# A gather that also waits until the third gather ahead of it has landed

## The chip, the core and the metric

The kernel runs on one core of a Trainium2 chip. A core has five engines with instruction streams of their own: TensorE (PE, matrix products; PEld is its weight load), VectorE (DVE), ScalarE (ACT), GpSimd (POOL) and SyncE (SP), which only issues transfers here. They tell each other of finished work through semaphores. Sixteen DMA engines move data between HBM and the on-chip memory; they are shared by all transfers, whoever issued them. A transfer raises a semaphore when it has landed. The metric is the time of one execution on the device, in microseconds (us).

## The reference

The kernel computes one layer of attention over the edges of a graph with 12500 nodes and 212500 edges (sorted by target node), then a batch norm over the nodes, a residual and a layer norm. Cut to what matters:

```python
Q, K, V = (x @ W for W in (WQ, WK, WV))            # 12500 x 128, as 8 heads of 16
Eh = edge_attr @ WE                                # 212500 x 128
score = K[src] * Q[dst] / sqrt(16) * Eh            # rows of K by source, of Q by target
score = exp(clip(score.sum(per head), -5, 5))
msg = V[src] * score
h_attn = segment_sum(msg, dst) / (segment_sum(score, dst) + 1e-6)
h = x + h_attn
h = (h - mean) * rsqrt(var + 1e-5) * gamma + beta  # over the nodes
out = layernorm(x + h)                             # over the 128 features of a node
```

The edges' sources are in no order, so K[src] and V[src] have to be fetched row by row: for each edge 1 KB, the K row and the V row of its source beside each other.

## The kernel before, in words

**Tiles and groups.** The edges are cut into 1661 tiles of 128 and these into 208 groups of eight tiles (the last has five). A group is made of two halves of four tiles, one for each of two windows of 64 target nodes.

**The table.** A first stage computes K and V of all nodes on TensorE and writes them as a table `kvd` to HBM, one row of 1 KB per node. For the first eight groups x itself is gathered and projected, so that they need no table.

**The gathers.** `gather` (line 221) issues an indirect transfer on POOL: 128 row numbers from a column of `srcs`, 128 rows of `kvd`, one tile of a `slot` in the on-chip memory, 128 KB in all. One gather serves one tile. `load_kv` (line 296) puts the gathers of a group into the list `queued` once a slot is free, and `issue` (line 228) and `pace` (line 233) take them from there. In the steady loop `pace` makes the first of them wait for the last product that read the slot before; the others follow on POOL's queue. Each gather raises one of eight completion semaphores in turn, and each waits, before it starts, for the gather that used its semaphore last, the eighth ahead. Twelve of the groups get their last tile not by a gather but by 128 transfers of one row each from SP's queue (`fetch_rows`, line 270), eight rows in an iteration.

**The other transfers in the steady loop**, all from SP's queue: `load` (line 504) brings the edge attributes of a group, `ea`, 512 KB, four groups ahead, as soon as the products that read the buffer before (`eh_mm`, line 584) are done; `load_quad` (line 401) brings the target positions of four groups, `rbq`, in two transfers of 256 KB. Near the end `load_x` (line 488) brings x for the residual into slots that are no longer needed.

**The order.** The program writes the order of every engine by hand: the loop at line 842 calls one small function after the other for group g and its neighbours, and each engine runs its instructions in that order. For group g VectorE multiplies K in the slot by the turned product of Q and Eh (`products`, line 640), once for each half; each of the two instructions waits until the gathers of its tiles have landed. Then come the sums by head (line 647), clip and exp, and the message (`message`, line 662), after which the slot is free. TensorE adds the messages up by target node (line 679).

`steady[0] = True` (line 804) stands after the table is written and the first gathers have been issued, ahead of the loop over the attention groups.

Of the kernel before, what the change touches and what calls it, by code (L numbers as in the profile page):

```python
# [29 lines left out]
ROWS = P  # L30
FIRST_ROW = 8
LATE = 8
BATCH = 1
ROW_LAG = 2
SP_ROWS = 8
# [43 lines left out]
def gnn_kernel(  # L79
# [19 lines left out]
    nc = tc.nc  # L99
# [38 lines left out]
    srcs = consts.tile([P, T], I32, name="srcs")  # L138
# [65 lines left out]
    table = [False]  # L204
    steady = [False]
# [9 lines left out]
    def kv_view(g, t):  # L215
# [2 lines left out]
        KV[g] = lambda a, b, c, n=P: (v[:, a:b, c:c + n] if g not in by_row or b < G else  # L218
                                      by_row[g][:, :, c:c + n])

    def gather(out, table, e):
        return nc.gpsimd.indirect_dma_start(out=out, out_offset=None, in_=table,  # L222
                                            in_offset=bass.IndirectOffsetOnAxis(ap=srcs[:, e:e + 1], axis=0))


    queued = []
# [1 line left out]
    def issue(n=0):  # L228
        while len(queued) > n:
            f, *a = queued.pop(0)  # L230
            f(*a)

    def pace(step):
        if queued:
            f, *a = queued.pop(0)
            tc.add_manual_dep(f(*a).ins, step.ins.name,
                              mybir.DependencyInfo(mybir.DependencyClass.Sync, mybir.DependencyReason.DATA),
                              reason="pace")
# [57 lines left out]
    def load_kv():  # L296
        while free and pending and table[0]:
            g = pending.pop(0)
            i = free.pop(0)
            kv_view(g, (i, slot(i)))  # L300
            for j in range(sizes[g] - (g in by_row)):
                queued.append((gather, KV[g](j, j + 1, 0, 2 * P).rearrange("p a d -> p (a d)"), kvd,
                               starts[g] + j))
            if not steady[0]:
                issue()

    for g in range(nxg):
        if g % 2 == 0:
            PAIR[g // 2] = free.pop(0)
            t = slot(PAIR[g // 2])  # L310
        XG[g] = t[:, (g % 2) * G * P:(g % 2 + 1) * G * P].rearrange("p (g d) -> p g d", d=P)
        for j in range(G):
            queued.append((gather, XG[g][:, j, :], x, g * G + j))
# [38 lines left out]
    def within(f, g):  # L352
        return f(g) if 0 <= g < NG else None
# [55 lines left out]

    quads = range(-(-2 * LATE // RQ), sizes.count(G) // RQ)  # L410

# [20 lines left out]
    def norm_first():  # L432

        nc.vector.bn_aggr(pre[:, 1:3], stats[:, :NPRE, :])
        nc.vector.tensor_tensor(stats[:, NPRE - 1, 3:6], pre, npre, op=OP.mult)
# [406 lines left out]
    for g in range(NG - 2):  # L842
# [18 lines left out]
        within(q_mm, g + 4)  # L861
        if g < LATE + 4:
            issue()
        elif g % BATCH == 0:
            pace(SENT[g - 1])
# [26 lines left out]
        if g == NG - 5:  # L892
            assert done >= set(range(NPRE))
            norm_first()
        if g == LATE - 1:
            tps.close()
            late.append(tps.enter_context(tc.tile_pool(name="late", bufs=1)))
        if g == LATE - 2:
            free.append(NSLOT)
# [329 lines left out]
```

## Time and profile before

| | |
|---|---|
| time, median of 3 runs (lowest, highest) | 2130.77 us (2128.43, 2132.06) |
| the profiled execution: its time, its span | 2129.44 us, 2127.7 us |
| busy: TensorE, VectorE, ScalarE, POOL | 1710.7, 1590.3, 670.9, 1593.9 us |
| gathers from `kvd` on POOL | 1585, busy 1505.5 us |
| DMA: bytes, mean rate | 386.61 MB, 182 GB/s |
| DMA queues, share of 16 engines' span: gathers, SP's | 33.8%, 25.5% |

The span goes from the first to the last instruction of the program in the trace; the execution's own time is 1.7 us longer. "Busy" is the time in which an engine had an instruction at work, and it does not count waiting. A row of a group names the line, the engine, the operation, what it writes and reads and how often, then busy time and the mean of one in ns, then the engine's idle time just ahead of these instructions and what ended it; "issue" there means that no semaphore in the trace did. For a gather, POOL's busy time is the writing of the transfer's descriptors; the transfer itself runs later on the DMA engines. In a timeline a row gives start, duration, engine, line, operation, tiles and, in brackets, the idle time before it and what ended that.

### The profile page before, as it was taken

The numbers are of one execution on the slowest core, as the hardware profiler recorded it, in microseconds if no ns is written. First come the engines' busy times: TensorE is split into PE (matmuls) and PEld (weight loads), VectorE is DVE, ScalarE is ACT, GpSimd is POOL, SyncE is SP. The second block draws the span as 40 slices with busy tenths as digits, with TensorE's granted clock in tenths as the row PEclk, the third lists the DMA queues.
The fourth block names the chain that finished last, engine by engine and source line by source line (L and its number), as shares of the span: only waits on it lengthen the run. The fifth ranks groups of instructions, "written<-read, shape, count | busy, mean of one in ns | idle before, by whom it ended". The sixth has DMA issues, their size and how long they took to land. (4 is left out here: it accounts for less than half of the span.)

```text
span 2127.7 us, 34387 instructions
## 1 busy us (share of the span) xinstructions
PE 1710.7 (80%) x9414; PEld 1103.8 (52%) x9414; DVE 1590.3 (75%) x3593; ACT 670.9 (32%) x2688; POOL 1593.9 (75%) x1685
## 2 busy tenths in 40 slices
PE   8889999877787787777777887787787777877787
PEld 7566566544454454454444554455554444545456
DVE  4559999777777777777777777767777767777787
ACT  3344343322322322322322322223223223223226
POOL 7776777777777777777777777777777777777775
PEclk9999999999898999999999999998998999898999
DMA  9856666565565565565565565565555565565574
GB/s 302 285 183 186 203 195 198 175 176 167 164 182 170 176 175 166 169 182 172 169 176 173 168 177 165 177 174 168 176 175 167 174 176 167 174 178 163 180 236 130
DMA packets 175391, 386.61 MB, mean 182 GB/s; under 512 B 37518, under 2 KB 91831, under 8 KB 175191
## 3 DMA queue, kind: packets, MB, share of 16 engines
q0 software_dynamic: 78128, 212.05, 33.8%
q1 hardware_dynamic: 92900, 169.50, 25.5%
q10 hardware_dynamic: 4163, 2.78, 0.5%
q8 instruction: 78, 1.28, 0.2%
q14 instruction: 122, 1.00, 0.2%
HBM read 364.57 MB, written 19.63 MB: 181 GB/s over the span
## 5 line engine op out<-in xcount | busy, mean ns | idle before, releaser
L222 POOL DMA_INDIRECT slot<-kvd,srcs x1585 | 1505.5, 950 | 487.6 <-issue 460.5
L640 DVE TENSOR_TENSOR slot<-slot,ps_t 128x512 f32<-128x512 f32 (+1 forms) x410 | 274.1, 677 | 423.0 <-DMA slot<-kvd,srcs 355.6
L622 PE MATMUL ps_t<-ident,wt 128*128 128x128 f32 x1661 | 282.3, 312 | 361.6 <-DVE wt L614 358.7
L679 PE MATMUL ps_a<-msg,oh 128*128 128x136 f32 (+1 forms) x3322 | 527.1, 298 | 1.7 <-DVE msg L662 1.7
L622 PEld LDWEIGHTS ps_t<-ident,wt 128*128 128x128 f32 x1661 | 211.3, 159 | 537.3 <-issue 472.5
L679 PEld LDWEIGHTS ps_a<-msg,oh 128*128 128x128 f32 (+1 forms) x3322 | 427.7, 171 | 81.1 <-issue 53.9
L657 ACT ACTIVATE ps_m<-s 128x64 f32<-128x64 f32 (+1 forms) x209 | 47.5, 227 | 1097.3 <-DVE s L656 1003.6
L589 PE MATMUL ps_e<-ea,w_e 128*128 128x512 f32 x832 | 390.6, 591 | 0.7 <-ACT wt L596 0.7
L614 DVE TENSOR_TENSOR wt<-wt,ps_q 128x512 f32<-128x512 f32 x416 | 264.3, 675 | 2.6 <-PE ps_q L604 2.6
L647 DVE TENSOR_REDUCE s<-slot 128x64 f32<-128x1024 f32 (+2 forms) x208 | 246.3, 1185 | 0.1
L662 DVE TENSOR_TENSOR msg<-slot,ps_m 128x1024 f32<-128x1024 f32 (+3 forms) x209 | 246.0, 1179 | 0.3 <-ACT ps_m L657 0.3
L596 ACT ACTIVATE wt<-ps_e 128x512 f32<-128x512 f32 x416 | 233.8, 620 | 12.1 <-PE ps_e L589 12.0
L604 PE MATMUL ps_q<-ot,q 64*128 64x512 bf16 x1248 | 209.7, 451 | 0.0
L589 PEld LDWEIGHTS ps_e<-ea,w_e 128*128 128x128 f32 x832 | 142.6, 190 | 100.4 <-issue 98.5
L542 DVE TENSOR_TENSOR oh<-ps_m,rel_i 128x512 f32<-128x512 f32 x208 | 141.0, 678 | 10.8 <-PE ps_a L679 10.8
L570 ACT ACTIVATE q<-qs 128x128 bf16<-128x128 f32 x208 | 64.4, 309 | 214.9 <-PE ps_q L604 180.3
L704 PEld LDWEIGHTS ps_a<-ident,at 128*128 128x128 f32 x408 | 71.3, 218 | 110.4 <-ACT q L577 53.4
L704 PE MATMUL ps_a<-ident,at 128*128 128x128 f32 x408 | 114.3, 367 | 2.5 <-DVE relrow L396 2.3
L709 ACT ACTIVATE hx<-ps_a 128x64 f32 x408 | 88.0, 216 | 44.4 <-PE ps_a L679 37.5
L531 ACT ACTIVATE xw<-hx 128x64 f32 x416 | 88.1, 280 | 11.2 <-DMA kvd<-slot 6.5
L604 PEld LDWEIGHTS <-q 64*128 64x128 bf16 x1248 | 48.5, 102 | 79.0 <-issue 61.6
L562 PE MATMUL ps_a<-w_q,xw 128*128 128x128 f32 x416 | 88.9, 299 | 0.6 <-ACT qs L566 0.4
(180 smaller groups left out, 1632.0 us busy)
## 6 DMA issues: line engine op xcount, KB each, us to landing
ea<-eaT SPq DMA_DIRECT2D x207, 512.0 KB
slot<-kvd,srcs POOLq DMA_INDIRECT x1585
byrow<-kvd SPq DMA_DIRECT2D x1536, 1.0 KB
rbq<-relT SPq DMA_DIRECT2D x94, 256.0 KB
kvd<-slot SPq DMA_DIRECT2D x12, 512.0 KB
kvd<-t SPq DMA_DIRECT2D x12, 512.0 KB
slot<-xT SPq DMA_DIRECT2D x24, 256.0 KB
out<-o SPq DMA_DIRECT2D x23, 256.0 KB
```

The source lines that it names most:

```text
L222: return nc.gpsimd.indirect_dma_start(out=out, out_offset=None, in_=table, in_offset=bass.IndirectOffsetOnAxis(ap=srcs[:, e:e + 1], axis=0))
L542: nc.vector.tensor_tensor(one, iota_ps[:, None, :].to_broadcast([P, n, P]), r[:, :n, None].to_broadcast([P, n, P]), op=OP.is_equal)
L589: nc.tensor.matmul(eh, w_e, EA[g][:, a:b, :].rearrange("p a b -> p (a b)"), start=True, stop=True)
L596: nc.scalar.activation(t[:, :(b - a) * P], EH[g][h], AF.Copy)
L604: nc.tensor.matmul(QE[g][h], Q3[g][r, k, :], OT[g][r, :(b - a) * P], start=(k == 0), stop=(k == 2))
L614: nc.vector.tensor_tensor(t, t, QE[g][h], op=OP.mult)
L622: nc.tensor.transpose(ps[:, j, :], WT[g][h][:, j * P:(j + 1) * P], ident)
L640: step = nc.vector.tensor_tensor(kv, kv, PW[g][i][:, c - a:d - a, :], op=OP.mult)
L647: step = nc.vector.tensor_reduce(SS[g][:, a:b, :], KV[g](a, b, 0).rearrange("p t (h d) -> p t h d", d=DH), axis=AX.X, op=OP.add)
L662: step = nc.vector.tensor_tensor(MSG[g][:, a:b, :P].rearrange("p t (h d) -> p t h d", d=DH), KV[g](a, b, P).rearrange("p t (h d) -> p t h ...
L679: nc.tensor.matmul(AGG[g][WN if j >= n else 0:], OH[g][j], MSG[g][:, j, :], start=(j == 0), stop=(j == n - 1))
L704: nc.tensor.matmul(ps, AT[g], ident, start=True, stop=False)
```

## The change

`gather` keeps a list `flight` of the gathers issued since `steady` was set. From the fourth on, each gets a dependency on the one three places ahead in that list: it may start only when that one's data has landed. So at most three gathers are under way at a time. Nothing else is changed: the same instructions in the same order on every engine, the same transfers.

```diff
 LATE = 8
+FLIGHT = 3
...
+    flight = []
+
     def gather(out, table, e):
-        return nc.gpsimd.indirect_dma_start(out=out, out_offset=None, in_=table,
-                                            in_offset=bass.IndirectOffsetOnAxis(ap=srcs[:, e:e + 1], axis=0))
+        d = nc.gpsimd.indirect_dma_start(out=out, out_offset=None, in_=table,
+                                         in_offset=bass.IndirectOffsetOnAxis(ap=srcs[:, e:e + 1], axis=0))
+        if steady[0]:
+            flight.append(d)
+            if len(flight) > FLIGHT:
+                tc.add_manual_dep(d.ins, flight[-1 - FLIGHT].ins.name,
+                                  mybir.DependencyInfo(mybir.DependencyClass.Sync, mybir.DependencyReason.DATA),
+                                  reason="in flight")
+        return d
```

In the built program the new dependency takes the place of the wait on the eighth gather ahead, which it implies; the first five gathers that carry it keep both.

## The prediction

> **What bounds the kernel now.** I read the page first (busy time, groups, chain), then the groups of the gather line by its tile, then the waits, and last the timeline around single gathers.
>
> ```profile
> span 2127.7 us, 34387 instructions
> PE 1710.7 (80%) x9414; PEld 1103.8 (52%) x9414; DVE 1590.3 (75%) x3593; ACT 670.9 (32%) x2688; POOL 1593.9 (75%) x1685
> ...
> ACT 1%; PE 1%; DVE 0%; issue 0%; DMA 0%; POOL 0%; DVEq 0%; ACTq 0%
> ...
> L222 POOL DMA_INDIRECT slot<-kvd,srcs x1585 | 1505.5, 950 | 487.6 <-issue 460.5
> L640 DVE TENSOR_TENSOR slot<-slot,ps_t 128x512 f32<-128x512 f32 (+1 forms) x410 | 274.1, 677 | 423.0 <-DMA slot<-kvd,srcs 355.6
> ...
> ea<-eaT SPq DMA_DIRECT2D x207, 512.0 KB
> ...
> rbq<-relT SPq DMA_DIRECT2D x94, 256.0 KB
> ```
>
> ```profile
> L222 POOL DMA_INDIRECT slot<-kvd,srcs x1585: 942/946/1141, 83.3 to 2075.2; - x199
> ```
>
> ```profile
> POOL slot L222 <- issue: 475.4, 1560, 0.3
> ...
> DVE slot L640 <- DMA slot<-kvd,srcs: 355.6, 155, 6.8
> ```
>
> No engine is over 80% busy, and the chain on the page breaks off after a few per cent (its shares add up to 2), so it cannot name the bound. The gather line can. Its 1585 gathers start between 83.3 and 2075.2 us: 1991.9/1584 = 1.257 us from start to start. One takes 950 ns, and ahead of 1560 of them POOL is idle for 475.4/1560 = 0.30 us that no semaphore ends ("issue"). 0.95 + 0.30 = 1.25: POOL goes from gather to gather without waiting for anyone, for 94% of the span. The 75% is 0.95/1.257, an engine that is never free. VectorE in turn waits for the gathers (355.6 us, 155 times), TensorE for VectorE. So whatever delays a gather's start on POOL moves the end by as much; after the last gather 2127.7 - 2075.2 = 52.5 us of tail remain, which the change does not touch.
>
> **The change: what it adds.** No instruction, no transfer and no byte. In the instruction streams each gather of before already waits for the one eight ahead of it (eight completion semaphores in turn). In the changed stream this wait names the semaphore of the third ahead; only the first five carry both. So the 0.30 us between gathers, in which a wait is looked at already, gets no extra wait to look at: cost nothing by itself. Two edges would be a gather's own longer decoding (none seen) and the wait being open. The gathers before the first attention group (64 of x and the first 16 of K and V) keep their old order.
>
> **When the wait is open.** The third gather ahead started 3 x 1.25 = 3.75 us earlier. What counts is how long a gather takes from start to landing. VectorE shows it: its product L640 starts when the last gather of its four-tile half has landed.
>
> ```profile
> 387.62 0.94 POOL L222 DMA_INDIRECT slot<-kvd,srcs  x1 [0.30 <-issue]
> ...
> 390.47 0.69 DVE L640 TENSOR_TENSOR slot<-slot,ps_t 128x512 f32<-128x512 f32 x1 [2.65 <-DMA slot<-kvd,srcs]
> ...
> 577.02 0.95 POOL L222 DMA_INDIRECT slot<-kvd,srcs  x1 [0.30 <-issue]
> 577.37 0.36 SPq L507 DMA_DIRECT2D ea<-eaT  x1
> ...
> 581.25 0.69 DVE L640 TENSOR_TENSOR slot<-slot,ps_t 128x512 f32<-128x512 f32 x1 [1.85 <-DMA slot<-kvd,srcs]
> ...
> 555.89 1.25 SPq L405 DMA_DIRECT2D rbq<-relT  x2
> 556.96 0.94 POOL L222 DMA_INDIRECT slot<-kvd,srcs  x1 [0.31 <-issue]
> 564.12 0.69 DVE L640 TENSOR_TENSOR slot<-slot,ps_t 128x512 f32<-128x512 f32 x1 [6.09 <-DMA slot<-kvd,srcs]
> ...
> 750.13 0.94 POOL L222 DMA_INDIRECT slot<-kvd,srcs  x1 [0.30 <-issue]
> 750.19 1.25 SPq L405 DMA_DIRECT2D rbq<-relT  x2
> 755.85 0.69 DVE L640 TENSOR_TENSOR slot<-slot,ps_t 128x512 f32<-128x512 f32 x1 [1.08 <-DMA slot<-kvd,srcs]
> ...
> 1028.56 1.24 SPq L405 DMA_DIRECT2D rbq<-relT  x2
> 1029.65 0.95 POOL L222 DMA_INDIRECT slot<-kvd,srcs  x1 [0.30 <-issue]
> 1036.25 0.69 DVE L640 TENSOR_TENSOR slot<-slot,ps_t 128x512 f32<-128x512 f32 x1 [2.00 <-DMA slot<-kvd,srcs]
> ```
>
> (Which gather a product waits for: counted in eights from the last gather of the kernel, one less for each group that gets its last tile row by row.) With nothing beside it a gather has landed 390.47 - 387.62 = 2.85 us after its start: 0.9 us before the third after it wants to start, wait closed. Beside one ea load it took 4.23 us; beside an ea load and the two rbq loads behind it 7.16, 5.72 and 6.60 us, 6.5 in the mean.
>
> ```profile
> 1046.00:1047.25 1.25, 1.25 (x8) 0.71 (x7) 0.00 (x0) 0.00 (x0) 0.95 (x1) 1.00 0.36 105
> 1049.75:1051.50 1.75, 0.31 (x3) 0.34 (x4) 1.72 (x6) 1.32 (x7) 1.37 (x2) 1.00 0.85 267
> 1069.75:1074.25 4.50, 4.09 (x31) 3.11 (x32) 4.04 (x10) 2.25 (x9) 3.37 (x4) 1.00 1.00 284
> ```
>
> These three stretches (the last two columns are the DMA engines' busy share and GB/s) say why. A lone gather uses 0.36 x 1.25 = 0.45 us of the 16 engines. An ea load fills them for some 1.75 us (share 0.85), an ea load with two rbq loads for 4.5 us (share 1.00). A gather whose packets come behind such a block waits for it.
>
> How late after a landing does POOL start? The one true wait of a gather in the trace:
>
> ```profile
> 176.59 1.22 DVE L662 TENSOR_TENSOR msg<-slot,ps_m 128x1024 f32<-128x1024 f32 x1
> 178.07 0.94 POOL L222 DMA_INDIRECT slot<-kvd,srcs  x1 [4.87 <-DVE msg L662]
> ```
>
> 176.59 + 1.22 = 177.81, and 178.07 is 0.26 us later. The landings above are read at VectorE's start, which itself lies between 0 and some 0.26 us behind them, so the wait opens for landings read as longer than something between 3.75 - 0.26 = 3.49 and 3.75. I take 3.6, the middle.
>
> **The sum.** One block of loads stops POOL once: later gathers have come later, find the block gone, and one gather's 0.45 us is shorter than the 1.25 us between starts, so the queue drains.
> - rbq blocks: 94 loads, two to a block, so 47 blocks. 6.5 - 3.6 = 2.9 us by the three rows. Those have a gather in the worst place; with at most three in flight instead of five (6.5/1.25), there is also about one gather less (0.45 us) ahead in the queue. I take 2.5: 47 x 2.5 = 118 us.
> - ea loads without rbq: 207 - 47 = 160. The first gather to meet the block is late by 0.5 to 1.75 us (a gather comes every 1.25 us), so it lands after 3.35 to 4.60 us, in which the row of 4.23 lies. Over 3.6 this is 0 to 1.0 us, in the mean 1.0 x 1.0/(2 x 1.25) = 0.40: 160 x 0.40 = 64 us.
> - The last groups also load the residual's x, 25 loads of up to 256 KB in about six bursts:
>
> ```profile
> L494 SPq DMA_DIRECT2D slot<-xT x25: 327/424/1303, 2008.2 to 2066.9; - x25
> ```
>
>  At 2 us, a little under an rbq block: 6 x 2 = 12 us.
>
> Together 194 us. Nothing hides it: POOL has no idle time that the 0.30 us does not need. Behind a waiting gather stand the other gathers of its group and those of the next one, on POOL's queue; for them waits VectorE (L640), and for VectorE the transposes of TensorE and with them the release of ea buffers, so the next loads on SyncE's queue move back by about the same. TensorE and ScalarE lose nothing of their own; they wait longer. The profiled execution took 2129.4 us (span 2127.7): 2129.4 + 194 = 2323. The median of the runs, 2130.77, lies 1.3 us above that execution: 2325.
>
> **Weighed against the pages.** The row: landings of 2.85 us alone and 4.23 to 7.16 us beside loads. The Trainium skill, "DMA: Bandwidth & Descriptors", section "Anatomy of one DMA — SWDGE (gpsimd) path", gives a DMA of POOL's queue as 2.0 us plus its bytes by 436 GB/s, which is an estimate of 2.3 us for 128 KB whatever runs beside it; by that the wait would never be open and the time would stay. The trace agrees for a lone gather only, roughly. The same page, "Queues, rings and completion order", has each DMA engine take turns between queues packet by packet. By fair turns a gather beside a load would need about twice its 0.45 us, land after some 3.3 us, and again the wait would stay closed. The 4.23 us and 6.60 us speak against fair turns.
>
> **Rivals.**
> 1. The wait is never open (fair turns of the queues, or a dependency that ends up without force): 2131. For it: the lone landing of 2.85 us leaves 0.9 us. Against: the three landings over 5.7 us; of the 155 waits of VectorE the longest is 6.8 us.
> 2. The blocks shrink: fewer gathers in flight let the loads through sooner, so an rbq block costs 1.5 us, an ea load 0.25, an x burst 1: 47 x 1.5 + 160 x 0.25 + 6 = 116 us, 2247. For it: the gathers in a block use engine time that the loads then get. Against: in the 4.5 us at 284 GB/s 1278 kB move, and the three loads alone are 1049 kB of them, so without any gather the block still lasts some 3.7 us.
> 3. The blocks always catch a gather at the worst place, since POOL and the loads now move in step: 3.3 us for an rbq block (7.16 less 3.6, less 0.26 for VectorE's own start), 0.6 for an ea load, 3 for an x burst: 155 + 96 + 18 = 269 us, 2400.
> 4. Faster: the gathers write their descriptors undisturbed when fewer transfers run, each takes the shortest 942 ns instead of 950: 1585 x 0.008 = 12.7 us, 2118. It decides only where no landing goes beyond 3.5 us, since one rbq block in ten (5 x 2.5 = 12.5) eats it up. Against: the minimum and the median, 942 and 946 ns, lie together; there is little to win.
>
> **How the numbers follow.** My forecast has 0.66, rival 2 0.14, rival 3 0.12, rival 1 0.05, rival 4 0.03. Rivals 2 and 3 are the same mechanism with the ends of its prices; the range takes in both and a little beyond, 2235 to 2410, and leaves out rivals 1 and 4 and the far tails. About 0.2% is what a measurement of this kernel can tell from no change: faster 0.03, same 0.05, slower 0.92.
>
> **What would show it.** In the profile after: the group of the gather line keeps 950 ns but its idle time goes from 487.6 to some 680 us, the surplus named as waiting for the gather's own landing, 150 to 300 times, none over about 4 us. VectorE's wait for gathers grows by about the same from 355.6. Busy times of all engines stay. Between loads the gathers stay 1.25 us apart. Wrong would be: start to start longer than 1.25 us everywhere, which would make the wait itself costly (0.05 us more on 1566 gathers is 78 us); stalls beside ea loads over 1 us; or gathers that land after 2.85 us beside the loads too.

## The result, and the profile after

The changed kernel took 2383.02 us (median of 4 runs, 2376.3 to 2386.0) against 2129.82 us (4 runs, 2128.43 to 2132.06) for the kernel before: a ratio of 1.1185, with a 95% interval of 1.1172 to 1.1199. The forecast was 2325 us with a range of 2235 to 2410: the sign, the place and the range held, the middle was 58 us too low.

First the page of the kernel after: span, busy times, and the groups of the gather and of the VectorE product that waits for it (gather's line now 225, product's now 650).

```profile
span 2381.5 us, 34392 instructions
...
PE 1780.0 (75%) x9414; PEld 1145.7 (48%) x9414; DVE 1592.1 (67%) x3593; ACT 667.8 (28%) x2688; POOL 1592.0 (67%) x1685
...
L225 POOL DMA_INDIRECT slot<-kvd,srcs x1585 | 1503.6, 949 | 742.1 <-issue 398.4
...
L650 DVE TENSOR_TENSOR slot<-slot,ps_t 128x512 f32<-128x512 f32 (+1 forms) x410 | 276.2, 678 | 674.3 <-DMA slot<-kvd,srcs 589.0
```

The span grew by 2381.5 - 2127.7 = 253.8 us. POOL's idle time just ahead of the gathers grew by 742.1 - 487.6 = 254.5 us, and a gather still takes 949 ns. So the whole loss stands on POOL between two gathers, which is where the prediction had put it; it is only 254 us instead of 194.

The same gathers by their tile, and the waits (engine, what waited, for what; us in total, times, longest):

```profile
L225 POOL DMA_INDIRECT slot<-kvd,srcs x1585: 940/946/1217, 83.5 to 2327.9; - x199
```

```profile
DVE slot L650 <- DMA slot<-kvd,srcs: 589.0, 184, 8.2
...
POOL slot L225 <- issue: 414.9, 1301, 2.9
POOL slot L225 <- DMA slot<-kvd,srcs: 330.2, 317, 4.0
```

Where before no gather stood beyond the usual 0.30 us for another one, 317 now wait for one, for 330.2 us (0.30 us of each is the old pause), none longer than 4.0 us. VectorE's wait for the gathers grew from 355.6 to 589.0 us, 233 us of the 254. The median gather is as before, 946 ns. After the last gather 2381.5 - 2327.9 = 53.6 us remain, against 52.5.

Two stretches of the timeline show the two kinds of stall. First an rbq block:

```profile
1010.32 0.95 POOL L225 DMA_INDIRECT slot<-kvd,srcs  x1 [0.30 <-issue]
1010.75 0.37 SPq L517 DMA_DIRECT2D ea<-eaT  x1
...
1011.18 1.25 SPq L415 DMA_DIRECT2D rbq<-relT  x2
...
1011.57 0.95 POOL L225 DMA_INDIRECT slot<-kvd,srcs  x1 [0.30 <-issue]
...
1012.83 0.95 POOL L225 DMA_INDIRECT slot<-kvd,srcs  x1 [0.30 <-issue]
...
1015.34 0.94 POOL L225 DMA_INDIRECT slot<-kvd,srcs  x1 [1.57 <-DMA slot<-kvd,srcs]
...
1017.92 0.94 POOL L225 DMA_INDIRECT slot<-kvd,srcs  x1 [1.64 <-DMA slot<-kvd,srcs]
...
1019.59 0.94 POOL L225 DMA_INDIRECT slot<-kvd,srcs  x1 [0.72 <-DMA slot<-kvd,srcs]
...
1020.83 0.94 POOL L225 DMA_INDIRECT slot<-kvd,srcs  x1 [0.30 <-issue]
```

The gather of 1015.34 waits for the third ahead of it, that of 1010.32, and so on down the rows. By the records of their semaphores the three awaited gathers landed at 1015.08, 1017.66 and 1018.82, which is 4.76, 6.09 and 6.00 us after their starts. The first two stalls end 0.26 us after the landing, the third 0.76 us after it, since the gather of 1019.59 is the first of a group and carries a second wait (below). What each start has over the usual 0.30 us is lost: 1.27 + 1.34 + 0.42 = 3.03 us for this block. Then an ea load alone:

```profile
1032.16 0.96 POOL L225 DMA_INDIRECT slot<-kvd,srcs  x1 [0.30 <-issue]
1032.64 0.36 SPq L517 DMA_DIRECT2D ea<-eaT  x1
...
1033.43 0.94 POOL L225 DMA_INDIRECT slot<-kvd,srcs  x1 [0.30 <-issue]
...
1034.67 0.94 POOL L225 DMA_INDIRECT slot<-kvd,srcs  x1 [0.30 <-issue]
...
1036.70 0.94 POOL L225 DMA_INDIRECT slot<-kvd,srcs  x1 [1.08 <-DMA slot<-kvd,srcs]
1037.94 0.95 POOL L225 DMA_INDIRECT slot<-kvd,srcs  x1 [0.30 <-issue]
```

Of the gathers shown only that of 1032.16 is late: landed at 1036.70 - 0.26 = 1036.44, 4.28 us after its start. The one stall costs 1.08 - 0.30 = 0.78 us, and the next start is 1.24 us on, as ever.

**The stalls counted.** I took every gather's idle time beyond 0.30 us and set it against the moment at which the records of its semaphore show the awaited gather landed. Three kinds come out. 248 stalls (197 us) end 0.26 us after that landing. 43 (42 us) end 0.76 us after it: all belong to gathers that carry a second wait, for VectorE, as the first gather of a group does. 16 (20 us) end for no reason that the trace shows, mostly 1.74 us after the landing; 15 of them are every 106th gather (numbers 49, 155, 261 and so on, counted from zero). The next table splits these 260 us. A late landing goes to the ea or rbq load that was issued last before it, from the first x load (2245.8 us) on to the x loads, and to none where less than 40 KB of SP's transfers ran beside the awaited gather. Where a stall can be counted to the load before or after, the rbq blocks get up to 8 us more and the ea loads as much less.

| term | prediction, us | trace, us |
|---|---|---|
| rbq blocks | 47 x 2.5 = 118 | 110 (96 stalls) |
| ea loads alone | 160 x 0.40 = 64 | 92 (156 stalls) |
| x loads at the end | 12 | 12 (11 stalls) |
| late landings with no load beside them | 0 | 9 (28 stalls) |
| second wait on a stalled gather, 0.5 us each where it shows | 0 | 17 |
| every 106th gather | 0 | 20 |
| sum | 194 | 260 |

The wait of 4.87 us at 178.07 in the kernel before, 4.6 us over the usual, has no counterpart after: 260 - 4.6 = 255, beside 254.5 on the page.

### The profile page after: what moved, and what is told of

Read it like the earlier page. It is cut to its first block, busy times and chain, and to the rows that moved or that the text cites. A ratio compares the mean times of both kernels' runs of the same rounds, so it can differ in the third digit from the quotient of the medians.

```text
span 2381.5 us, 34392 instructions
## 1 busy us (share of the span) xinstructions
PE 1780.0 (75%) x9414; PEld 1145.7 (48%) x9414; DVE 1592.1 (67%) x3593; ACT 667.8 (28%) x2688; POOL 1592.0 (67%) x1685
## 5 line engine op out<-in xcount | busy, mean ns | idle before, releaser
L225 POOL DMA_INDIRECT slot<-kvd,srcs x1585 | 1503.6, 949 | 742.1 <-issue 398.4
L650 DVE TENSOR_TENSOR slot<-slot,ps_t 128x512 f32<-128x512 f32 (+1 forms) x410 | 276.2, 678 | 674.3 <-DMA slot<-kvd,srcs 589.0
L632 PE MATMUL ps_t<-ident,wt 128*128 128x128 f32 x1661 | 307.0, 334 | 548.7 <-DVE wt L624 548.0
L632 PEld LDWEIGHTS ps_t<-ident,wt 128*128 128x128 f32 x1661 | 231.2, 170 | 726.9 <-issue 674.6
L689 PEld LDWEIGHTS ps_a<-msg,oh 128*128 128x128 f32 (+1 forms) x3322 | 433.0, 174 | 81.4 <-issue 53.8
L614 PE MATMUL ps_q<-ot,q 64*128 64x512 bf16 x1248 | 231.8, 491 | 0.0
L714 PEld LDWEIGHTS ps_a<-ident,at 128*128 128x128 f32 x408 | 77.7, 237 | 124.2 <-issue 78.0
L714 PE MATMUL ps_a<-ident,at 128*128 128x128 f32 x408 | 123.1, 392 | 2.5 <-DVE relrow L406 2.3
L715 PE MATMUL ps_a<-xw,ident 128*128 128x128 f32 x408 | 93.9, 318 | 0.0
```

Of the source, the lines that this page charges most:

```text
L225: d = nc.gpsimd.indirect_dma_start(out=out, out_offset=None, in_=table, in_offset=bass.IndirectOffsetOnAxis(ap=srcs[:, e:e + 1], axis=0))
L614: nc.tensor.matmul(QE[g][h], Q3[g][r, k, :], OT[g][r, :(b - a) * P], start=(k == 0), stop=(k == 2))
L632: nc.tensor.transpose(ps[:, j, :], WT[g][h][:, j * P:(j + 1) * P], ident)
L650: step = nc.vector.tensor_tensor(kv, kv, PW[g][i][:, c - a:d - a, :], op=OP.mult)
L689: nc.tensor.matmul(AGG[g][WN if j >= n else 0:], OH[g][j], MSG[g][:, j, :], start=(j == 0), stop=(j == n - 1))
L714: nc.tensor.matmul(ps, AT[g], ident, start=True, stop=False)
```

## The experiments

My theory when they were made: POOL bounds, and the loss is the sum of gathers that land late because of SP's big loads. The rivals: the loss does not hang on the loads but on the number in flight or on the wait itself (the 0.76 us and the 106th gathers speak for a part of that).

### Eight runs on two chips where the kernel before took over 3000 us

These eight kernels met two chips on which the kernel before itself took 3029 to 3164 us (three runs, beside the first four kernels) and 3131 to 3226 us (13 runs, beside the others). So their times cannot be set against the rest; what I read from them is POOL's rows.

One gather more in flight, and one fewer:

```diff
-FLIGHT = 3
+FLIGHT = 4
```

> Four gathers under way instead of three, all else as in the changed kernel. Theory (a gather starts at the later of 1.25 us after the one before it and 0.26 us after the landing of the one that it waits for; landings keep their length): the wait is open for landings over 4 x 1.25 - 0.26 = 4.74 us instead of 3.49. Nearly only the blocks with rbq loads reach that; their 2.5 us fall by 1.25 to some 1.3 (47 x 1.3 = 61 us), ea loads alone to about 0.1 (16 us): 2130 + 75 to 110, so 2205 to 2240 us. Rival (the wait costs every gather something, 254/1566 = 0.16 us): still about 2383 us.

Measured: 3019.53 and 3083.17 us; POOL waited for a gather's landing 31 times, 31.3 us.

```diff
-FLIGHT = 3
+FLIGHT = 2
```

> Two gathers under way. Theory: now the wait is open for every gather, since a lone one lands after 2.73 us and two starts are only 2.50 us apart. Two gathers per 2.73 + 0.26 = 2.99 us: 1.49 us each instead of 1.25, 1566 x 0.24 = 376 us; to that the loads. If the loads move along with the gathers and each landing keeps its length, they cost about 600 us more (some 3100 us); if a block of loads passes while POOL stands, about 270 us more (some 2780 us). Rival (a fixed cost of the wait): about 2383 us.

Measured: 3011.15 us. The wait on POOL:

```profile
POOL slot L225 <- DMA slot<-kvd,srcs: 1130.7, 1116, 5.4
```

With two in flight the wait is open for 1116 of 1585 gathers, since a lone landing already takes longer than two starts; with four it is open for 31. The counts fall as 1116, 317, 31, the middle one from the usual chip. That is the order expected, but it is no measure of time, and with four in flight POOL also stood 727.1 us for VectorE's messages, in which gathers could land. No run on a usual chip had another number in flight than three or the eight of the kernel before.

The changed kernel without the later rbq loads (old target positions are used again, so this part of the data is left out):

```diff
     def load_quad(q):
+        if q >= quads[2]:
+            for k in range(RQ):
+                RB[RQ * q + k] = RB[RQ * (q - 2) + k]
+            return
```

> The changed kernel without the rbq loads after the first two quads: later groups read the positions of a group eight before, which leaves out part of the data and changes no instruction of the five engines. Theory: the trace of the changed kernel puts 118 us of POOL's standing beside the 47 blocks with rbq loads; without those loads a block is one ea load as elsewhere, which costs 0.8 us: 2383 - 118 + 47 x 0.8 = 2303 us (2285 to 2320). Rival (a fixed cost of the wait): 2383 us.

Measured: 2925.94 us; POOL waited for landings 86 times, 75.3 us.

The changed kernel without the later ea loads (old edge attributes are used again):

```diff
     def load(g):
+        if g >= 12:
+            EA[g] = EA[g - 3]
+            return
```

> The changed kernel without the ea loads from group 12 on: later groups read the edge attributes of an earlier one, which leaves out that part of the data; the rbq loads stay. Theory: the 126 us beside the ea loads alone go, and an rbq block is shorter by the 2.1 us that an ea load fills the engines, so its 2.5 us fall to about 0.6: 2383 - 126 - 47 x 1.9 = 2168 us (2150 to 2200). Rival (a fixed cost): 2383 us.

Measured: 2998.75 us; 44 times, 42.7 us.

Both edits in the changed kernel, and both in the kernel before (edge attributes and target positions of the later groups are left out in each):

```diff
+        if q >= quads[2]:
...
+        if g >= 12:
...
```

> The changed kernel without the later ea and rbq loads (positions and edge attributes of earlier groups are read again, the data of the later ones left out). Theory: a lone gather lands 2.73 us after its start, the wait closes at 3.49, so POOL goes from gather to gather again; what stays is the x loads of the end, 15 us, and a few stalls beside the single rows: 2140 to 2155 us. Rival (a fixed cost of the wait): 2383 us. Rival (TensorE's lower granted clock makes the kernel longer): the time follows the clock, not the loads.

> The kernel before without the later ea and rbq loads (the same data left out). Theory: POOL's start-to-start time of 1.25 us is the bound of the kernel before and these loads delay nobody: 2130 us, within 0.3%. If the loads cost the kernel before something through the DMA engines, it gets faster.

Measured: 3095.93 us with 18 waits for landings of 13.8 us, and 3102.77 us. They are 0.988 (0.967 to 1.010) and 0.984 (0.975 to 0.992) of the kernel before on that chip: even without the later loads and without the new wait little was regained, and the waits of that last kernel say why it is no measure:

```profile
POOL slot L222 <- DVE msg L669: 877.1, 98, 18.1
ACT hx L716 <- remote: 766.7, 62, 18.8
DVE oh L549 <- remote: 612.6, 55, 16.7
```

POOL waits for VectorE's messages, and VectorE and ScalarE stand for up to 18.8 us at a time for something that the profile ties to no instruction ("remote"). TensorE's mean granted clock was 0.758 there, against 0.920 for the kernel before on its usual chip, while a gather took 948 ns as ever. POOL alone was not the bound there, so a delay on POOL can be hidden. On time, these runs decide nothing.

A second wait on every gather of a group, on a step of VectorE that is long done, in the changed kernel and in the kernel before:

```diff
     def issue(n=0):
         while len(queued) > n:
             f, *a = queued.pop(0)
-            f(*a)
+            d = f(*a)
+            if steady[0] and passed:
+                tc.add_manual_dep(d.ins, passed.pop(0).ins.name, ..., reason="second wait")
```

> The changed kernel in which every gather of a group also waits for an instruction of VectorE that ended long ago, as the first gather of a group does anyway: no new reason to stand, only a second semaphore to look at. Theory from the trace of the changed kernel: a gather with one wait starts 0.26 us after the landing, one with two waits 0.76 us after it, and a wait that is closed costs nothing. So the 248 stalls of gathers with one wait get 0.5 us more each (124 us), and landings between 2.99 and 3.49 us become stalls too (about 25 us): 2383 + 150 = 2530 us (2490 to 2570). Rival: a second wait costs its 0.5 us on every gather, open or not: 2383 + 1385 x 0.5 = 3075 us. Rival: it costs nothing: 2383 us.

> The kernel before with the same second wait on every gather. Theory: the sequencer looks at the waits of later gathers while POOL is at work on an earlier one, and no wait is open, so it costs nothing: 2130 us within 0.3%. Rival (a second wait costs 0.5 us on every gather): 2130 + 690 = 2820 us.

Measured: 2691.73 and 2711.25 us, which is 0.859 (0.840 to 0.878) and 0.865 (0.860 to 0.870) of the kernel before on that chip. In the second of them the second wait is the only difference, and its slowest run (2716.14) lies under the fastest of the kernel before (3131.05), so on that chip it made the kernel faster. That it holds POOL back and so spreads the transfers is a guess; the cause stays open. On a usual chip the same edit of the changed kernel did the opposite (below).

### The ea load cut in two

```diff
-        nc.sync.dma_start(EA[g][:, :n, :]..., eaT[...])
+        m = n if g < 12 else U
+        nc.sync.dma_start(EA[g][:, :m, :]..., eaT[...])
...
         within(message, g)
+        if g + 4 < NG:
+            load_half(g + 4, SENT[g])     # the other half, after group g's message
```

> The changed kernel with each ea load cut in two of 256 KB, the second issued after the message of the group, about half a group later: the same bytes in shorter blocks. Theory: the length of a block decides. Half a load fills the engines for about 1.1 us; a gather behind it lands after at most 2.73 + 1.1 = 3.8 us, so the 126 us of the ea loads alone fall to some 20, and the rbq blocks lose about 1 us each: 2383 - 106 - 47 = 2230 us (2200 to 2290). Rival (the bytes decide, not the block): 2383 us.

Measured: 2373.92 us (2368.89 to 2378.95) against 2131.4, a ratio of 1.1138 (1.1107 to 1.1168). Expected were about 2230, so this was a miss, and the timeline and the waits say why:

```profile
1020.13 0.37 SPq L524 DMA_DIRECT2D ea<-eaT  x1
...
1020.61 0.36 SPq L518 DMA_DIRECT2D ea<-eaT  x1
```

```profile
POOL slot L225 <- DMA slot<-kvd,srcs: 306.8, 313, 3.2
```

Line 524 is the second half of one group, line 518 the first half of the next. SP's queue is in order: the first half of the next group stood behind the waiting second half, and both went out 0.48 us apart as one block of 512 KB. So do nearly all: 185 of 196 second halves have the next first half within 0.6 us. The waits are almost those of the change (313 against 317). The length of a block was not varied, so the run doesn't tell what a shorter block costs; I had not asked what the moved transfer holds up on its own queue.

### Twelve gathers fewer in the kernel before

```diff
-SP_ROWS = 8
+SP_ROWS = 16
```

More groups get their last tile row by row from SP, and POOL has 12 gathers fewer.

> The kernel before with 16 rows instead of 8 fetched row by row on SyncE's queue in an iteration, so that about 24 groups instead of 12 get their last tile without a gather. Theory (POOL's gathers bound the kernel before): 12 gathers fewer, 12 x 1.257 = 15 us: 2115 us. Rival (something else is the bound or the row transfers slow the others): 2130 us or more.

Measured: 2117.05 us (5 runs, 2114.8 to 2121.0) against 2131.4, a ratio of 0.9940 (0.9925 to 0.9955).

```profile
span 2113.0 us, 37497 instructions
```

```profile
L222 POOL DMA_INDIRECT slot<-kvd,srcs x1573: 942/946/1299, 83.5 to 2060.1; - x197
```

12 x 1.257 = 15.1 us was to be had if POOL is the bound, and 14.35 us came, though 3110 instructions were added on other engines. Start to start is (2060.1 - 83.5)/1572 = 1.257 us, as before. So the number of gathers on POOL sets the time, and not the instructions of the others or the bytes (386.8 MB here, 386.6 before); and this version is 0.6% faster than the kernel before.

### The changed kernel without the later ea and rbq loads, on a usual chip

The edits are those shown above, both together; edge attributes and target positions of the later groups are left out. The ea loads of the first 12 groups, four rbq loads and the 25 x loads stay.

```diff
+        if q >= quads[2]:
...
+        if g >= 12:
...
```

> The changed kernel without the later ea and rbq loads once more, beside a kernel before that runs at its usual 2130 us (data of the later groups left out as before). Theory (the loads make the gathers land late, the wait itself is free): 2140 to 2160 us, POOL's wait for its own landings at most some 30 us of the 330 us of the changed kernel. Rival (the wait costs every gather 0.16 us, whatever else runs): 2383 us. Between the two, about 2150 + 40, if second waits and the refilling of POOL's instruction stream cost something without any late landing too.

Measured: 2197.77 us (2195.08 to 2200.47) against 2132.95, a ratio of 1.0305 (1.0274 to 1.0336). Page, waits, and two places of the timeline:

```profile
span 2198.7 us, 33877 instructions
...
L225 POOL DMA_INDIRECT slot<-kvd,srcs x1585 | 1504.3, 949 | 557.8 <-issue 461.2
```

```profile
POOL slot L225 <- issue: 476.4, 1514, 2.8
...
POOL slot L225 <- DMA slot<-kvd,srcs: 83.7, 99, 2.6
```

```profile
1032.69 0.94 POOL L225 DMA_INDIRECT slot<-kvd,srcs  x1 [0.67 <-DMA slot<-kvd,srcs]
...
1037.43 0.94 POOL L225 DMA_INDIRECT slot<-kvd,srcs  x1 [1.30 <-DMA slot<-kvd,srcs]
```

Of the loss of some 250 us, 2383.02 - 2197.77 = 185 us go with the loads. This carries the theory, but 65 us stay over the kernel before, where a kernel without late landings would have come back to it. POOL's idle time (557.8 - 487.6 = 70.2 us over that of before) divides into 42 us of late landings, 16 us of second waits and 17 us at every 106th gather, less the stall at 178.07. Of the 42 us some 20 belong to the loads that stay: 11 before 210 us and 9 at the x loads. The other 22 us (67 stalls) lie between 210 and 2066 us, where no load runs. So gathers land late even with no load beside them. The DMA queues between 1033.5 and 1037 us, ahead of the stall of 1037.43 (queue: packets, MB, share of the 16 engines):

```profile
q0 software_dynamic: 104, 0.30, 30.6%
q8 instruction: 1, 0.02, 2.9%
```

Beside the gathers (q0) there is one packet of the engines' own instruction streams (q8), which occupies one DMA engine for 2.9% x 16 x 3.5 = 1.6 us. A gather raises its semaphore sixteen times (1541 of 1585 gathers in the changed kernel's trace have all sixteen records), as often as there are DMA engines, and has landed only with the last of these. Between 250 and 2000 us 368 gathers had such a packet beside them, on queue q8 (16 KB each) or q14 (8 KB each), and 91 of them landed later than 3.3 us after their start; of the 990 gathers with none, one did, and 98% landed within 2.88 us. All 67 stalls between 210 and 2066 us awaited a gather with such a packet. The page counts these packets for the whole run (packets, MB, share):

```profile
q8 instruction: 78, 1.28, 0.2%
q14 instruction: 119, 0.97, 0.1%
```

There are 197 of them, and 99 waits on POOL. This is a coincidence of time in 91 of 92 cases and not an experiment: a kernel with the same gathers and fewer instructions wasn't tried.

### A second wait on every gather, on a usual chip

The edit of the second wait shown above, in the changed kernel.

```diff
+            if steady[0] and passed:
+                tc.add_manual_dep(d.ins, passed.pop(0).ins.name, ..., reason="second wait")
```

> The changed kernel in which every gather of a group also waits for an instruction of VectorE that ended long ago, beside a kernel before that runs at its usual 2130 us. Theory from the trace of the changed kernel: with one wait a gather starts 0.26 us after the landing, with two 0.76 us after it, closed waits cost nothing; and POOL's instruction stream, now with one more instruction per gather, is refilled every 55 to 60 gathers instead of every 106, which shows as a stall of some 1.3 us each time. 248 x 0.5 = 124 us for the stalls there are, some 20 us for landings between 2.99 and 3.49 us, 12 more refills x 1.3 = 15 us: 2383 + 159 = 2542 us (2500 to 2590). Rival (a second wait costs 0.5 us on every gather): 2383 + 1385 x 0.5 = 3075 us. Rival (it costs nothing, and the 0.76 us have another cause): 2383 us.

Measured: 2515.94 us (2514.51 to 2517.37) against 2132.93, a ratio of 1.1795 (1.1761 to 1.1829); 133 us more than the change alone.

```profile
span 2512.7 us, 35751 instructions
...
L225 POOL DMA_INDIRECT slot<-kvd,srcs x1585 | 1504.0, 949 | 873.1 <-DMA slot<-kvd,srcs 274.3
```

```profile
1033.89 0.94 POOL L225 DMA_INDIRECT slot<-kvd,srcs  x1 [0.63 <-DVE qs L590]
1035.26 0.94 POOL L225 DMA_INDIRECT slot<-kvd,srcs  x1 [0.43 <-DMA slot<-kvd,srcs]
1036.51 0.95 POOL L225 DMA_INDIRECT slot<-kvd,srcs  x1 [0.30 <-DVE oh L561]
```

A hit: 342 of its 375 stalls end 0.76 us after the landing, and 2 end 0.26 us after it. A second wait costs 0.5 us wherever the first one is open and nothing where both have passed: the gather of 1036.51, with two waits, starts after the usual 0.30 us. (The row names VectorE at 1033.89 although that step was long done; the time went to the landing.) 35751 - 34392 = 1359 instructions came, one for each wait that was added: an instruction that only waits stands ahead of the gather. The Trainium skill, "Perfetto Trace Analysis", section "Identifying Dependency Chains", says that an instruction with waits on several engines may get an event-semaphore instruction with the additional wait ahead of it. By that sentence the count of instructions agrees; what it costs isn't there, and is 0.5 us here.

One expectation failed: if the extra stalls of the 106th gathers hung on the number of instructions, they had to come every 55 to 60 gathers now. They came at the same gathers as before, numbers 49, 155 and 261. So they go by the number of gathers. What comes round every 106 gathers was not found.

What fits a refilling of POOL's instruction stream does show in this run, elsewhere and smaller than expected. Every 64th gather (numbers 57, 121, 185 and so on), which is every 128 instructions of gather and wait, has an 8 KB packet of q14 within 0.35 us of its start in 21 of 24 cases, against 4% of all gathers. 19 of the 24 start 1.05 to 1.07 us after the landing, 0.30 us more than the other stalls. The gather of 1035.26 above is one of them.

## Why the prediction was right or wrong

**What bounds the kernel: right.** The span's 253.8 us are POOL's 254.5, and the kernel with 12 gathers fewer returned 14.35 of 15.1 us.

**"Between loads the gathers stay 1.25 us apart", and a closed wait is free: right.** 1301 gathers still start after "issue": 414.9 us, which is 0.30 us each and some 20 us of the extra stalls. A gather takes 949 ns for 950; the longer decoding, one edge of that step, did not come.

**"Cost nothing by itself": the step that failed as put.** It held for a closed wait only. An open wait adds its 0.26 us from landing to start, which the prediction had taken from the one true wait of the trace, and it was right for 248 stalls. But a gather with a second wait starts 0.76 us after the landing. In the kernel before that was the first gather of a group, and its price could not be seen, since the wait for the eighth ahead was never open. It is 17 us. The prediction looked at the five gathers to which the change gave a second wait, and not at the gathers that had one already. The stalls of every 106th gather, 20 us, belong to the same step: in the kernel before nothing is to be seen at those gathers.

**The rbq blocks: right in size, 110 for 118.** 110/47 = 2.34 us by landings alone, with the 2.5 taken. "One block of loads stops POOL once" did not hold in the block shown: POOL stops twice for late landings and once more for a second wait. For the size of the loss the sum over a block counts, and the last late landing sets it.

**The ea loads: the term that was mis-sized, 92 for 64.** The price of a load was too low. An ea load fills the engines for 2.15 us from its first to its last packet (median of 136), where the prediction took 1.75 us from one load's window. The 157 ea loads alone ahead of the x loads cost 0.51 us each where no packet of an instruction stream ran beside the load (110 of them), against 0.40 forecast, and 0.77 us where one did (47). So 157 x 0.51 = 80 us are the loads' own, and 12 us more come with the instruction streams. How a gather's delay follows from the length of a block stays open: with 2.15 us, 2.73 us for a lone gather and 3.49 us for the open wait, the prediction's own formula would give 0.77 us for a load, more than was measured. "Stalls beside ea loads over 1 us" were named as a sign of error: 16 of 156 are, up to 2.36 us, the median is 0.62.

**Late landings without a load: 9 us, put at nothing.** In all 28 cases a packet of an instruction stream ran beside the awaited gather. With the 12 us beside ea loads that is 21 us, and the kernel without the later loads has 22 us of this kind. The page's list of queues gives these transfers 0.2% and 0.1% of the engines' time. That they cause the delay is argued from the coincidence in time, in two traces, and not shown by a run that changes them.

**The x loads: 12 for 12.** The price was a guess from the rbq blocks, 2 us for each of six bursts, so that the match is in part luck; it came as 11 stalls.

**"Busy times of all engines stay": wrong for TensorE,** 1710.7 to 1780.0 us with the same 9414 products, at a mean granted clock of 0.881 after 0.920. Across the kernels on a usual chip the clock falls with POOL's standing: 0.920 before, 0.908 without the loads, 0.881 for the change, 0.852 with the second wait. TensorE is not the bound (75% busy), and POOL's idle time explains the span without it. Why the clock falls was not tested.

**The rivals.** Rival 1 (never open) fell with 317 waits. Rival 4 (faster) fell with it: the shortest gather went from 942 to 940 ns. Rivals 2 and 3 gave the ends of the prices: an rbq block cost neither 1.5 nor 3.3 us but 2.34; an ea load, 92/157 = 0.59 us with the instruction streams, came to rival 3's 0.6. The time lies between the forecast and rival 3 (2400), mostly for terms that neither had: second waits, every 106th gather and late landings without a load, 46 us together. That they fit under the upper end of the range is luck, since that end was set by rival 3's prices for the loads.

**The pages.** A gather with nothing beside it has landed 2.73 us after its start, by the records of its semaphore, while its row lasts 0.95 us. The Trainium skill, "Perfetto Trace Analysis", section "DMA Instruction — SWDGE (GPSIMD)", says that the profiler's end of such an instruction is the writing of the last descriptor and not the arrival of the data. The trace agrees: 0.95 us of POOL, 1.8 us more until the data are there. The 3.3 us of fair turns, which the prediction weighed against its rows, don't come here either: gathers landed 4.76 to 6.09 us after their starts beside the rbq block shown. But that estimate takes the turns to be short, and the section that it draws on, the Trainium skill, "DMA: Bandwidth & Descriptors", section "Queues, rings and completion order", says that an engine drains a whole packet, typically 9 to 17 descriptors, before it switches. An ea load has 128 rows of 4 KB in the trace, eight for each of 16 engines if they are spread evenly. If those eight are one packet, a gather behind them waits for the whole load, as it does here; no run here shows where the packets end. So the rows speak against short turns and not against that section.

**The sum corrected by what was measured:** 110 + 92 + 12 + 9 + 17 + 20 - 4.6 = 255 us; 2129.4 + 255 = 2384, beside 2383.02 measured.

## What to carry to other kernels

Run-ahead of a transfer queue is worth what the longest landings need, not what a lone one does: 2.73/1.25 asks for three gathers in flight, 7/1.25 for six, and three cost 11.9% (six is this arithmetic, no run had it). When the engine that issues is the bound, price a wait by the cases in which it is open, count the other waits that the same instruction carries, and look at every user of the DMA engines, those with 0.2% of the time too: a gather that ends with the last of sixteen landings can be late by one packet on one engine. A transfer that is held back on an in-order queue holds what stands behind it, so a load isn't split by making its second half wait.

## What the runs showed that was not expected

- From a landing to POOL's start 0.26 us pass with one wait and 0.76 us with two (342 of 375 stalls where every gather has two), and nothing is added where both have passed.
- Every 106th gather starts some 1.74 us after the awaited landing, 3.34 us or more with second waits, with nothing in the trace that explains it; in the kernel before, with eight gathers of run-ahead, nothing shows there. It goes by the count of gathers and not of instructions; the cause is open.
- With a second wait on every gather, every 64th gather starts 0.30 us later still after its landing, with an 8 KB packet of an instruction stream beside its start in 21 of 24 cases.
- 91 of 92 late landings in the kernel without the later loads have an instruction-stream transfer of 8 or 16 KB beside them, up to 1.6 us on one DMA engine; a quarter of all its gathers have one.
- On one chip, where the kernel before took 3131 to 3226 us, the second wait cut that kernel's time by 13.5% (to 2711.25, for a cause that stays open); on a usual chip it made the changed one 5.6% slower (2515.94/2383.02).
- TensorE's mean granted clock fell with POOL's standing, from 0.920 to 0.881 and 0.852, for the same products.
